# A two-layer network on one core: a first norm shared with VectorE, memsets spread over turns, and a reordered end with spread gathers, earlier additions and a reordered last batch

## The chip, the core and the metric

The kernel runs on one core of a Trainium2 chip. Five engines work side by side, each with its own instruction queue that runs in order: PE (TensorE, matrix products; its weight loads are listed as PEld), DVE (VectorE), ACT (ScalarE), POOL (GpSimd, which also issues the indirect gathers and scatters) and SP (SyncE, which here only issues DMAs). Engines wait for each other through semaphores. The metric is the device time of one execution in microseconds (us); a comparison uses the median of several runs.

## The reference

The input `x` has 16 sequences of 512 tokens with 128 features, all in float32.

```python
xn = layernorm(x)
x = x + memory0(xn) + ffn0(xn)
xn = layernorm(x)
x = x + attention1(xn) + experts1(xn)
```

- `memory0` cuts the sequences into 8 chunks of 64 tokens. Three gate weights give per chunk `alpha`, `theta`, `eta` (a product of each chunk's 64 x 128 values with a 3-column weight). A two-layer memory is trained through the 8 chunks, one after the other, by gradient steps with clipping, and then read by all tokens.
- `ffn0` is a convolution, attention with 16 heads, a norm, 8 experts applied to all tokens and weighted by a softmax, and a norm.
- `attention1` is causal attention with 16 heads, whose output goes through a convolution and becomes the queries of a second causal attention over the same keys and values.
- `experts1` routes each token to 8 of 32 experts; each expert takes the first 128 tokens that chose it, and its weighted outputs are added to those tokens.

## The kernel before

**Turns.** The order of the work is written out by hand. Every stage (the norm, the training scan, one batch's front, one slot's first or second pass over the scores, the experts) is a Python generator, and `Turns.run` advances each live stage by one step per turn, in order of priority (0 first). A stage is listed with the turn in which it begins, and it also waits for marks that others leave (`after`, `mark`), for locks (`acquire`), for free score slots or value tiles (`take`), and for room among three shared PSUM tiles (`room`, `hold`, `drop`). PE's instructions run exactly in that order; on the other engines the framework may reorder what doesn't depend. `fill` adds idle-time products at the end of a thin turn. What matters for the time is thus how many turns there are and how long each takes.

**Attention.** `tops` is the first pass over the scores of one slot (a slot has half the heads of a batch): scores on PE, row maxima on DVE (L387, L395, L396), in the lock `p1`. `back` is the second: scores again with the maxima subtracted, exponential on ACT (L461), in layer 1 the causal mask on POOL (L465), and the product with the values (`pc`), in the lock `p2`. In layer 1 each takes 11 turns per slot, there are four slots a batch (two rounds of two), and a new batch begins every 44 turns (`TBB`). `between(b)` makes the second round's queries from the first round's result. `last(b)` makes the attention's output `xo` and stores it in `ao[b]`.

**The head.** `norm0` normalizes the 16 batches, one begun per turn: `moments` (statistics on DVE, `rsqrt` on POOL, L203 and L204), the scaling in `layernorm` on POOL (L226, four instructions a batch), a transposition into `xnT` on PE, and a store to `xt[0]`. Then the gates: `pg` adds up 64 products, each with 128 columns of `xnT` (every 64th token) as the weights and three columns of `w3` as the moving side. Before all this, three score slots (`qx` zeroed on DVE, L628; `kx` set to one on POOL, L313) and two value tiles (`vp`, L302) are set up. `front0(b)` loads `xt[0, b]` and makes queries, keys and values of layer 0.

**The order after it.** The scan of the memory follows norm0 and must end before layer 1 begins; layer 1 counts its turns from `t0 = max(turns.turn, 480)`. When the routing of the last batch is done, `moe` begins: a placement (four products `pt` over a table of counts, with several DVE instructions each), 32 gathers of a row of counts per expert (L1279) with a count on DVE, and 16 pairs of experts. `fetch` loads a pair's weights on SP and gathers its tokens on POOL (L1314); `pair` runs them through the expert and scatters the result with addition into `acc` in DRAM (L1356), two scatters in one turn. When all pairs are done, `total(b)` loads `acc` and `ao` of each batch (L1381, L1383), adds them on POOL (L1385) and stores the output (L1386), as soon as `ao[b]` is there. The tiles of `total` share a ring of three buffers (tag `hTe`, two tiles a batch); the tiles of `last` share a ring of two (tag `st`) with `front1` and `between`.

Of the kernel before, what the change touches and what calls it, by code (L numbers as in the profile page):

```python
# [82 lines left out]
def network(ctx: ExitStack, tc: tile.TileContext, a, out):  # L83
# [83 lines left out]
    def drop():  # L167

        read[0] += 1
# [49 lines left out]

    def layernorm(dst, src, gain=None, shift=None):  # L220

        got = []
        yield from moments(src, got)
        mv, rs = got[0]
        for t in range(TB):
            nc.gpsimd.tensor_scalar(  # L226
                dst[:, t, :], src[:, t, :], mv[:, t, 0:1], rs[:, t : t + 1], ALU.subtract, ALU.mult
            )
# [71 lines left out]
    def padded_values(pool, i):  # L300
        vp = pool.tile([P, TB, HEADS, 32], F32, bufs=1, name=f"vp{i}")
        nc.gpsimd.memset(vp, 0.0)  # L302
# [4 lines left out]
        return vp  # L307

    def key_rows(pool, i):


        kx = pool.tile([P, NH, S], FR, bufs=1, name=f"kx{i}")
        nc.gpsimd.memset(kx.bitcast(F32), 1.0)  # L313
        return kx

# [308 lines left out]

    def score_slot(pool, i):

        q = pool.tile([P, NH, S], FR, bufs=1, name=f"qx{i}")
        nc.vector.memset(q.bitcast(F32), 0.0)  # L628
        return q, key_rows(pool, i), topd[i]

    free_slots = [score_slot(att, i) for i in range(3)]
    free_values = [padded_values(att, i) for i in range(2)]
    th = const.tile([P, NT, NC], F32, name="th")
# [9 lines left out]
    def norm0(p0):  # L643
# [5 lines left out]
        C0 = Pack(load(p0, "const0", [P, sum(CONST0.values())]), CONST0)  # L649
        xnT = p0.tile([P, N], F32, bufs=1, name="xnT")  # L650

        def one(b):
            xb = p0.tile([P, TB, D], F32, tag="xb", bufs=8, name="xb")
            nc.sync.dma_start(xb, x_b[b])
            yield from layernorm(xb, xb)
            yield from room()
            transpose_tokens(xnT[:, b * S : (b + 1) * S], xb)
            nc.sync.dma_start(xt[0, b], xnT[:, b * S : (b + 1) * S])
            mark("xn", b)
            yield  # L660
# [4 lines left out]
        yield from room()  # L665
        pg = hold("pg")
        for t in range(CHUNK):
            mm(pg[:, 0:3], x_bct[:, :, t], w3[:, t, :], start=(t == 0), stop=(t == CHUNK - 1))
            if t % 8 == 7:
                yield  # L670
        g3 = p0.tile([P, 3], F32, bufs=1, name="g3")
        nc.vector.tensor_copy(g3, pg[:, 0:3])
        drop()
        gr = p0.tile([P, 80], F32, bufs=1, name="gr")
# [340 lines left out]
    def front0(b):  # L1015
        z = live[0, b] = {}
        yield from after(("xn", b))
        xT = fa.tile([P, S], F32, tag="st", bufs=2, name="xT")
        nc.sync.dma_start(xT, xt[0, b])
        yield from idle(2)  # L1020
# [79 lines left out]
    )  # L1100
    with tc.tile_pool(name="p0", bufs=1) as p0:
        stage = norm0(p0)
        turns.stages.append((0, 3, ends(stage, "norm0")))
        turns.run(until=lambda: ("norm0",) in done)
# [9 lines left out]
    row.update(load_rows(l1, "rowsB", ROWSB), caus=C1("caus"), tri=C1("tri"))  # L1114
    free_slots.append(score_slot(l1, 3))
    free_values.append(padded_values(l1, 2))
    pools["pairs"] = False

# [95 lines left out]
    def last(b):  # L1214
# [14 lines left out]
        drop()  # L1229
        nc.sync.dma_start(ao[b], xo)  # L1230
        mark("ao", b)
        yield

    istar = mw.tile([P, EXP1], F32, name="istar")
    base = mw.tile([P, EXP1], F32, name="base")
# [3 lines left out]
    def moe(mo):  # L1239
# [10 lines left out]
        per = 512 // NTILE  # L1250
        for u in range(EXP1 // per):
            es = slice(u * per, (u + 1) * per)
            bd = ff.tile([EXP1, per, NTILE], F32, tag="ew1", bufs=2, name="bd")
            nc.vector.tensor_tensor(bd, bc(cur, 1, per), bc(memE[:, es], 2, NTILE), ALU.mult)
            yield from room()
            pt = work("pt")
            mm(pt, ones[0:EXP1, :], bd.rearrange("k e i -> k (e i)"))
            ptv = pt.rearrange("p (e i) -> p e i", i=NTILE)
            le = ff.tile([P, per, NTILE], F32, tag="ew2", bufs=2, name="le")
            nc.vector.tensor_scalar(le, ptv, col("iota"), None, ALU.is_le)  # L1260
            nc.vector.tensor_reduce(istar[:, es], le, AX.X, ALU.add)
            nc.vector.tensor_tensor(le, le, ptv, ALU.mult)
            nc.vector.tensor_reduce(base[:, es], le, AX.X, ALU.max)
            yield
        nc.vector.tensor_scalar(base, base, -1.0, col("iota"), ALU.mult, ALU.add)
# [11 lines left out]
        for e in range(EXP1):  # L1277
# [7 lines left out]
            if e >= 8:  # L1285
                count(e - 8)
            if e % 2 == 1:
                yield
        for e in range(EXP1 - 8, EXP1):
            count(e)  # L1290
        yield
        nc.vector.scalar_tensor_tensor(tok, istar, float(P), tok, ALU.mult, ALU.add)
# [12 lines left out]
        def fetch(e2):  # L1305
# [4 lines left out]
            nc.sync.dma_start(dn, a["dn"][:, es, :])  # L1310
            xg = mo.tile([P, 2, XW], F32, tag="xg", bufs=3, name="xg")
            for i in range(2):
                e = 2 * e2 + i
# [4 lines left out]
                )  # L1318
            return gu, dn, xg

        def pair(e2, gu, dn, xg):
# [19 lines left out]
            nc.vector.tensor_tensor(he, he, pgs[:, 1], ALU.mult)  # L1341
            yield
            yield from room()
            peo = toks(hold("peo")[:, 0 : 2 * D])
# [9 lines left out]
            for i in range(2):  # L1354
                e = 2 * e2 + i
                nc.gpsimd.indirect_dma_start(  # L1356
                    out=acc, out_offset=bass.IndirectOffsetOnAxis(ap=sidx[:, e : e + 1], axis=0),
                    in_=eo[:, i, :], in_offset=None,
                    bounds_check=N + P - 1, oob_is_err=True, compute_op=ALU.add,
                )  # L1360
            yield

        ahead = [fetch(0), fetch(1)]
        yield from idle(2)
        going = []
        for e2 in range(EXP1 // 2):
            going.append(pair(e2, *ahead.pop(0)))
            if e2 + 2 < EXP1 // 2:
                ahead.append(fetch(e2 + 2))
            for _ in range(3):  # L1370
                going = [g for g in going if next(g, StopIteration) is not StopIteration]
                yield
        while going:
            going = [g for g in going if next(g, StopIteration) is not StopIteration]
            yield
        mark("moe")

    def total(b):
        yield from after(("moe",), ("ao", b))
        x1 = ff.tile([P, TB, D], F32, tag="hTe", bufs=3, name="fin")  # L1380
        nc.sync.dma_start(x1, acc_b[b])  # L1381
# [133 lines left out]
```

## Time and profile before

| | |
|---|---|
| median of 3 runs | 4081.94 us |
| lowest, highest | 4064.09, 4087.86 us |
| the profiled execution | 4071.58 us |
| its span | 4069.8 us |
| mean granted PE clock | 0.952 |
| busy: PE | 3646.2 us (90%) |
| DVE | 2368.5 us (58%) |
| ACT | 2201.1 us (54%) |
| POOL | 1681.3 us (41%) |
| DMA traffic | 374.22 MB |

The span is what the profiler saw from the first to the last instruction; the execution's own time is 1.8 us more. A busy share is a mean over stages with different limits, so the stretches at the start and at the end are read by themselves: busy time per window, the timeline (each row: start, length, engine, line, operation, what is written and read, and in brackets how long the engine was idle before it and what ended that), and the chain of waits, which follows the last instruction back to what released it. The clock column is the share of full clock that PE was granted.

### The profile page before, as it was taken

The numbers are of one execution on the slowest core, as the hardware profiler recorded it, in microseconds if no ns is written. First come the engines' busy times: TensorE is split into PE (matmuls) and PEld (weight loads), VectorE is DVE, ScalarE is ACT, GpSimd is POOL, SyncE is SP. The second block draws the span as 40 slices with busy tenths as digits, with TensorE's granted clock in tenths as the row PEclk, the third lists the DMA queues.
The fourth block names the chain that finished last, engine by engine and source line by source line (L and its number), as shares of the span: only waits on it lengthen the run. The fifth ranks groups of instructions, "written<-read, shape, count | busy, mean of one in ns | idle before, by whom it ended". The sixth has DMA issues, their size and how long they took to land.

```text
span 4069.8 us, 62831 instructions
## 1 busy us (share of the span) xinstructions
PE 3646.2 (90%) x22668; PEld 1974.2 (49%) x22668; DVE 2368.5 (58%) x5165; ACT 2201.1 (54%) x3686; POOL 1681.3 (41%) x2598
## 2 busy tenths in 40 slices
PE   5998899888999998999999999999999999987877
PEld 2544454444544444455555555555555555543443
DVE  3575656665565555564566655666656666676651
ACT  1355655566557775555555555555555555542332
POOL 7334534455333544134333442333334423434563
PEclk6799999999999999999999999999999999997888
DMA  4222222122223333333333333333333343323334
GB/s 155 62 62 62 70 57 77 57 68 64 75 75 93 108 96 108 101 105 110 90 111 103 114 81 111 108 100 95 111 101 107 87 117 106 94 69 98 70 69 131
DMA packets 271222, 374.22 MB, mean 92 GB/s; under 512 B 42392, under 2 KB 116800, under 8 KB 270144
## 3 DMA queue, kind: packets, MB, share of 16 engines
q1 hardware_dynamic: 263744, 363.38, 30.7%
q0 software_dynamic: 7168, 6.82, 1.0%
q8 instruction: 180, 2.95, 0.3%
q14 instruction: 130, 1.06, 0.1%
HBM read 236.85 MB, written 133.25 MB: 91 GB/s over the span
## 4 chain that ended last, share of the span: by engine, by line
PE 62%; DVE 15%; POOL 7%; ACT 6%; DMA 5%; issue 5%; SPq 0%; POOLq 0%; ACTq 0%; DVEq 0%
PE s L190 16%; PE pye L573 10%; PE phe L190 9%; PE pc L190 9%; DVE nm L396 7%; DVE s L395 3%; ACT e L461 2%; PE pgr L190 2%; POOL e L465 1%; PE tp L241 1%; DVE s L387 1%; PE fill L197 1%; PE po L190 1%; PE pj L190 1%; DMA fin<-ao 1%
## 5 line engine op out<-in xcount | busy, mean ns | idle before, releaser
L461 ACT ACTIVATE e<-s 128x1024 f32<-128x1024 f32 (+1 forms) x1216 | 1190.6, 979 | 836.5 <-PE s L190 796.0
L396 DVE TENSOR_REDUCE nm<-s 128x2 f32<-128x1024 f32 (+1 forms) x704 | 861.9, 1224 | 664.6 <-PE s L190 657.5
L387 DVE CUSTOM_DVE_ANT_0 s<-s,sb_const 128x512 f32<-128x512 f32 (+1 forms) x1024 | 647.6, 632 | 663.9 <-PE s L190 646.4
L465 POOL TENSOR_SCALAR_AFFINE_SELECT e<-e 128x128 f32<-128x128 f32 (+2 forms) x1408 | 464.4, 363 | 1140.9 <-ACT e L461 1133.0
L190 PE MATMUL s<-kx,qx 64*128 64x512 f32 (+3 forms) x3072 | 627.6, 435 | 180.9 <-DVE nm L396 99.4
L190 PE MATMUL pc<-e,vp 128*32 128x512 f32 (+3 forms) x6144 | 712.4, 511 | 52.4 <-POOL e L465 51.3
L190 PEld LDWEIGHTS s<-kx,qx 64*128 64x128 f32 x3072 | 278.7, 189 | 754.0 <-issue 288.9
L573 PEld LDWEIGHTS pye<-ew,hTe 128*128 128x128 f32 x4096 | 517.2, 193 | 212.1 <-issue 195.6
L573 PE MATMUL pye<-ew,hTe 128*128 128x128 f32 x4096 | 572.7, 283 | 0.5 <-DVE cn L486 0.5
L190 PE MATMUL phe<-x1T,ew 128*128 128x512 f32 x1024 | 553.5, 624 | 6.9 <-DVE vp L345 1.9
L190 PE MATMUL s<-qx,kx 64*128 64x512 f32 (+3 forms) x3072 | 536.1, 373 | 21.1 <-ACT e L461 15.3
L565 ACT ACTIVATE hTe<-phe,sb_cols 128x512 f32<-128x512 f32 x512 | 353.1, 690 | 272.5 <-PE phe L190 272.1
L190 PEld LDWEIGHTS s<-qx,kx 64*128 64x128 f32 x3072 | 290.7, 190 | 124.2 <-issue 64.6
L581 POOL TENSOR_TENSOR ac<-ac,y 128x512 f32<-128x512 f32 x128 | 165.4, 1292 | 387.0 <-ACT y L580 386.8
L395 DVE TENSOR_TENSOR s<-s,sb_const 128x256 f32<-128x256 f32 (+1 forms) x384 | 199.4, 519 | 178.8 <-PE s L190 166.5
L190 PEld LDWEIGHTS pc<-e,vp 128*32 128x32 f32 x6144 | 137.6, 109 | 264.7 <-issue 152.2
L190 PEld LDWEIGHTS phe<-x1T,ew 128*128 128x128 f32 x1024 | 158.2, 193 | 113.3 <-issue 84.6
L580 ACT ACTIVATE y<-pye,pr 128x128 f32<-128x128 f32 x512 | 146.8, 368 | 51.0 <-PE pye L573 50.0
L387 DVE DVE_READ_ACCUMULATOR2_ANT nm<- 128x1 f32 x1024 | 145.0, 142 | 0.0
L197 PE MATMUL fill<-sb_pb,sb_const 128*128 128x512 f32 (+3 forms) x256 | 135.9, 621 | 8.8 <-DMA sb_pb<-in_pb 7.8
L437 ACT COPY cs<-pc 128x512 f32<-128x512 f32 x96 | 56.2, 585 | 61.1 <-PE pc L190 59.4
L410 ACT CAST m<-tpm 16x512 fp32r<-16x512 f32 x96 | 54.6, 569 | 59.4 <-PE tpm L408 59.4
(285 smaller groups left out, 4049.0 us busy)
## 6 DMA issues: line engine op xcount, KB each, us to landing
ew<-in_ew SPq DMA_DIRECT2D x256, 256.0 KB
kx<-rk SPq DMA_DIRECT2D x192, 256.0 KB
qx<-rq SPq DMA_DIRECT2D x128, 256.0 KB
rq<-hi SPq DMA_DIRECT2D x64, 256.0 KB
rq<-lo SPq DMA_DIRECT2D x64, 256.0 KB
rk<-hi SPq DMA_DIRECT2D x64, 256.0 KB
rk<-lo SPq DMA_DIRECT2D x64, 256.0 KB
qx<-r SPq DMA_DIRECT2D x64, 256.0 KB
```

The lines of the kernel that those rows point to most:

```text
L190: nc.tensor.matmul(o, lhsT=lhsT, rhs=rhs, start=start, stop=stop)
L197: nc.tensor.matmul(o[:, 0:n], lhsT=ident, rhs=cell[0][:, 0:n], start=True, stop=True)
L387: newest[0] = nc.vector.tensor_tensor_reduce(out=sv[:, r, 0, :], in0=sv[:, r, 0, :], in1=row["caus"][:, S - n :], scale=1.0, scalar=-BIG, ...
L395: nc.vector.tensor_tensor(dg, dg, bc(row["caus"][:, S - P :], 1, per), ALU.add)
L396: newest[0] = nc.vector.tensor_reduce(nm[:, qt, :, t : t + per], sv, AX.X, ALU.max)
L437: nc.scalar.copy(cs, got[0])
L461: nc.scalar.activation(e[:, :, 0 : per * n], s[:, :, 0 : per * n], AF.Exp, scale=SCALE)
L465: cleared[0] = nc.gpsimd.affine_select(out=ev[:, r, :, 0:P], in_=ev[:, r, :, 0:P], pattern=[[0, per], [1, P]], compare_op=ALU.is_ge, fill= ...
L565: nc.scalar.activation(hs[i], ph, AF.Relu, bias=col("fb", i))
L573: nc.tensor.matmul(pye[0][:, t, :], lhsT=h[:, t * P : (t + 1) * P], rhs=w2[e][:, f, :], start=(f == 0 and t == 0), stop=(f == 3), skip_gro ...
L580: nc.scalar.mul(y[:, t, :], pye[0][:, t, :], pr[:, t, e : e + 1])
L581: nc.gpsimd.tensor_tensor(ac, ac, y, ALU.add)
```

## The change

**Head.** The x loads of the first four batches are given priority over other loads. The scaling of the first norm runs on DVE for batches 0 to 3, and alternates between DVE and POOL for the others. The three slots and two value tiles are set up by stages that begin in turns 0, 8, 22 (slots 0, 1, 2: POOL, DVE, POOL) and 2, 24 (values), not before turn 0. `front0(0)` reads `xnT` in place. The gate product swaps its sides: `w3`'s three columns are the weights, and the 128 columns of `xnT` move; the result is copied, transposed back and copied. Slot 3, set up before layer 1, is set on POOL alone.

```diff
-    def layernorm(dst, src, gain=None, shift=None):
+    def layernorm(dst, src, gain=None, shift=None, on=None):
...
-            nc.gpsimd.tensor_scalar(
+            (on or (nc.gpsimd,))[t % len(on or (0,))].tensor_scalar(
...
+    def ready_slot(slot, on):
+        for t, value in zip(slot, (0.0, 1.0)):
+            on.memset(t.bitcast(F32), value)
+            yield
+        free_slots.append(slot)
+
+    fresh = [score_slot(att, i, (nc.gpsimd, nc.vector, nc.gpsimd)[i]) for i in range(3)]
+    fresh += [padded_values(att, i) for i in range(2)]
...
-            nc.sync.dma_start(xb, x_b[b])
-            yield from layernorm(xb, xb)
+            with ExitStack() as first:
+                if b < 4:
+                    first.enter_context(tc.high_priority())
+                nc.sync.dma_start(xb, x_b[b])
+            yield from layernorm(xb, xb, on=(nc.vector,) if b < 4 else (nc.vector, nc.gpsimd))
...
-        pg = hold("pg")
+        pg = hold("pg")[0:3, 0:P]
         for t in range(CHUNK):
-            mm(pg[:, 0:3], x_bct[:, :, t], w3[:, t, :], start=(t == 0), stop=(t == CHUNK - 1))
+            mm(pg, w3[:, t, :], x_bct[:, :, t], start=(t == 0), stop=(t == CHUNK - 1))
...
+        gT = p0.tile([3, P], F32, bufs=1, name="gT")
+        nc.scalar.copy(gT, pg)
+        drop()
+        yield
+        yield from room()
+        pgt = work("pg3")[:, 0:3]
+        nc.tensor.transpose(pgt, gT, ident[0:3, 0:3])
         g3 = p0.tile([P, 3], F32, bufs=1, name="g3")
-        nc.vector.tensor_copy(g3, pg[:, 0:3])
-        drop()
+        nc.vector.tensor_copy(g3, pgt)
...
+        turns.stages += [(t, 2, stage) for t, stage in zip((0, 8, 22, 2, 24), fresh)]
```

**Experts.** Each of the four placements becomes a stage of four steps, and the four start one turn apart. The gathers of counts come three in two turns where they came two in one, and the last eight counts in two turns. The gathers and the scatters of a pair come one a turn, and a pair has one more idle turn before its second product.

```diff
-        for u in range(EXP1 // per):
+        def places(u):
...
             nc.vector.tensor_tensor(bd, bc(cur, 1, per), bc(memE[:, es], 2, NTILE), ALU.mult)
+            yield
             yield from room()
-            pt = work("pt")
+            pt = hold("pt")
...
+            yield
             nc.vector.tensor_scalar(le, ptv, col("iota"), None, ALU.is_le)
             nc.vector.tensor_reduce(istar[:, es], le, AX.X, ALU.add)
+            yield
             nc.vector.tensor_tensor(le, le, ptv, ALU.mult)
+            drop()
             nc.vector.tensor_reduce(base[:, es], le, AX.X, ALU.max)
-            yield
+        yield from side(*[places(u) for u in range(EXP1 // per)])
...
-            if e % 2 == 1:
+            if e % 3 != 0:
                 yield
         for e in range(EXP1 - 8, EXP1):
             count(e)
-        yield
+            if e % 4 == 3:
+                yield
+        mark("counted")
...
             for i in range(2):
                 e = 2 * e2 + i
+                if i == 1:
+                    yield
                 nc.gpsimd.indirect_dma_start(
                     out=acc, out_offset=bass.IndirectOffsetOnAxis(ap=sidx[:, e : e + 1], axis=0),
```

**Additions.** A batch whose attention output is ready before `counted` is added to `acc` at once, and `total` then copies it from `acc` to the output, DRAM to DRAM.

```diff
-        nc.sync.dma_start(ao[b], xo)
+        if ("counted",) in done:
+            nc.sync.dma_start(ao[b], xo)
+        else:
+            x2 = l1.tile([P, TB, D], F32, tag="st", bufs=2, name="xs")
+            nc.sync.dma_start(x2, acc_b[b])
+            yield from idle(2)
+            nc.gpsimd.tensor_tensor(x2, x2, xo, ALU.add)
+            nc.sync.dma_start(acc_b[b], x2)
+            whole.add(b)
...
         yield from after(("moe",), ("ao", b))
+        if b in whole:
+            nc.sync.dma_start(out_b[b], acc_b[b])
+            return
```

**The last batch.** Its stages begin 12 to 24 turns earlier than its place in the row of batches, and so come into the list of stages before some of batches 13 and 14.

```diff
+    def begun(b, i, c):
+        early = 0 if b < B - 1 else 12 if i else 16 + 8 * c
+        return t0 + b * TBB + 20 + 66 * i + 11 * c - early
...
-        + [(t0 + b * TBB + 20 + 66 * i + 11 * c, 0, tops(1, b, i, c)) for b in range(B) for i in range(2) for c in range(2)]
-        + [(t0 + b * TBB + 40 + 66 * i + 11 * c, 1, back(1, b, i, c)) for b in range(B) for i in range(2) for c in range(2)]
-        + [(t0 + b * TBB + 60, 4, between(b)) for b in range(B)]
+        + [(begun(b, i, c), 0, tops(1, b, i, c)) for b in range(B) for i in range(2) for c in range(2)]
+        + [(begun(b, i, c) + 20, 1, back(1, b, i, c)) for b in range(B) for i in range(2) for c in range(2)]
+        + [(begun(b, 0, 0) + 40, 4, between(b)) for b in range(B)]
```

More of the change, by code (lines that the diff above doesn't have):

```diff
@@ L301, in padded_values, with ready_values @@
         vp = pool.tile([P, TB, HEADS, 32], F32, bufs=1, name=f"vp{i}")
+        return ready_values(vp)
+    def ready_values(vp):
         nc.gpsimd.memset(vp, 0.0)
@@ L306, in padded_values @@
             )
[L307 to L314, printed above, removed]
+        free_values.append(vp)
+        yield
     def split_rows(p, bias, order, dst):
@@ L623, in network, with score_slot @@
     row.update(load_rows(fa, "rows0", ROWS0))
-    def score_slot(pool, i):
+    free_slots, free_values = [], []
+    def score_slot(pool, i, on):
         q = pool.tile([P, NH, S], FR, bufs=1, name=f"qx{i}")
[L628 to L632, printed above, removed]
+        k = pool.tile([P, NH, S], FR, bufs=1, name=f"kx{i}")
+        return ready_slot((q, k, topd[i]), on)
+    def ready_slot(slot, on):
[5 more added lines that the diff above has]
+    fresh += [padded_values(att, i) for i in range(2)]
     th = const.tile([P, NT, NC], F32, name="th")
@@ L650, in norm0 @@
         xnT = p0.tile([P, N], F32, bufs=1, name="xnT")
+        live["xnT"] = xnT
         def one(b):
             xb = p0.tile([P, TB, D], F32, tag="xb", bufs=8, name="xb")
-            nc.sync.dma_start(xb, x_b[b])
-            yield from layernorm(xb, xb)
+            with ExitStack() as first:
[3 more added lines that the diff above has]
+            yield from layernorm(xb, xb, on=(nc.vector,) if b < 4 else (nc.vector, nc.gpsimd))
             yield from room()
@@ L1017, in front0 @@
         yield from after(("xn", b))
-        xT = fa.tile([P, S], F32, tag="st", bufs=2, name="xT")
-        nc.sync.dma_start(xT, xt[0, b])
-        yield from idle(2)
+        if b == 0:
+            xT = live["xnT"][:, 0:S]
+        else:
+            xT = fa.tile([P, S], F32, tag="st", bufs=2, name="xT")
+            nc.sync.dma_start(xT, xt[0, b])
+            yield from idle(2)
         yield from room()
@@ L1114, in network @@
     row.update(load_rows(l1, "rowsB", ROWSB), caus=C1("caus"), tri=C1("tri"))
-    free_slots.append(score_slot(l1, 3))
-    free_values.append(padded_values(l1, 2))
+    for _ in score_slot(l1, 3, nc.gpsimd):
+        pass
+    for _ in padded_values(l1, 2):
+        pass
     pools["pairs"] = False
@@ L1229, in last @@
         drop()
-        nc.sync.dma_start(ao[b], xo)
+        if ("counted",) in done:
+            nc.sync.dma_start(ao[b], xo)
+        else:
+            x2 = l1.tile([P, TB, D], F32, tag="st", bufs=2, name="xs")
+            nc.sync.dma_start(x2, acc_b[b])
+            yield from idle(2)
+            nc.gpsimd.tensor_tensor(x2, x2, xo, ALU.add)
+            nc.sync.dma_start(acc_b[b], x2)
+            whole.add(b)
         mark("ao", b)
         yield
+    whole = set()
     istar = mw.tile([P, EXP1], F32, name="istar")
@@ L1311, in fetch @@
             xg = mo.tile([P, 2, XW], F32, tag="xg", bufs=3, name="xg")
+            ahead.append((gu, dn, xg))
             for i in range(2):
@@ L1318, in fetch @@
                 )
-            return gu, dn, xg
+                yield
         def pair(e2, gu, dn, xg):
@@ L1342, in pair @@
             yield
+            yield
             yield from room()
@@ L1355, in pair @@
                 e = 2 * e2 + i
+                if i == 1:
+                    yield
                 nc.gpsimd.indirect_dma_start(
@@ L1361, in pair @@
             yield
-        ahead = [fetch(0), fetch(1)]
+        ahead, going = [], [side(fetch(0), fetch(1))]
         yield from idle(2)
[L1365 to L1373, printed above, removed]
+        at = e2 = 0
+        while going or e2 < EXP1 // 2:
+            if at % 3 == 2 and e2 < EXP1 // 2:
+                going.append(pair(e2, *ahead.pop(0)))
+                if e2 + 2 < EXP1 // 2:
+                    going.append(fetch(e2 + 2))
+                e2 += 1
             going = [g for g in going if next(g, StopIteration) is not StopIteration]
+            at += 1
             yield
```

## The prediction

> **What bounds it now.** The page first: one core, span 4069.8 us, execution 4071.58 us, against a median of 4081.94 us of three runs (4064.09 to 4087.86), so the sums below start 10 us under the median.
>
> ```profile
> PE   5998899888999998999999999999999999987877
> POOL 7334534455333544134333442333334423434563
> PEclk6799999999999999999999999999999999997888
> PE 62%; DVE 15%; POOL 7%; ACT 6%; DMA 5%; issue 5%; SPq 0%; POOLq 0%; ACTq 0%; DVEq 0%
> ```
>
> In the middle PE is busy nine tenths at nearly full clock; the change adds no PE work there. The first slice and a half and the last four have idle PE, low clock and busy POOL, and all edits but small ones lie there. The order of the code is in turns, and L461 issues one exponential per turn while a second pass runs: matching those rows with the walk of the stages dates every turn. Norm0 ends in turn 31 (132 us), the scan in 481, `xw` of batch 15 in 1167 (3680 us), `moe` in 1243 (3967 us), the last second pass in 1275.
>
> **The head.** Busy time by stretch (length, then busy us and count of PE, PEld, DVE, ACT, POOL; clock, DMA share, GB/s), then POOL's timeline:
>
> ```profile
> 16.00:88.00 72.00, 37.04 (x91) 16.99 (x91) 21.02 (x100) 10.57 (x18) 67.24 (x92) 0.55 0.44 143
> 92.00:131.00 39.00, 39.00 (x156) 32.92 (x156) 12.94 (x15) 0.30 (x2) 0.19 (x1) 0.50 0.15 46
> 84.15 0.19 POOL L203 TENSOR_SCALAR rs_t<-ln_mv 128x4 f32<-128x4 f32 x1
> 84.42 1.02 POOL L204 TENSOR_TENSOR ln_rs<-rs_t,nhalf 128x4 f32<-128x4 f32 x1
> 85.55 3.12 POOL L226 TENSOR_SCALAR xb<-xb,ln_mv,ln_rs 128x128 f32<-128x128 f32 x4
> ```
>
> Until 88.7 us POOL sets the pace: 4.6 us a batch. Then until 131 us PE does, in the gate product `pg`: eight turns of 16 passes, 3.56 us each lot in the chain, at half clock though it is busy all the time.
>
> **The tail.** The same columns, five stages:
>
> ```profile
> 3590.00:3680.00 90.00, 78.33 (x528) 36.47 (x528) 65.47 (x177) 41.16 (x50) 34.33 (x84) 1.00 0.29 83
> 3682.00:3713.00 31.00, 17.18 (x51) 5.52 (x51) 20.77 (x48) 3.37 (x5) 2.17 (x8) 0.56 0.21 55
> 3713.00:3781.00 68.00, 53.99 (x295) 23.14 (x296) 45.40 (x160) 22.23 (x26) 49.18 (x74) 0.87 0.33 83
> 3781.00:3965.00 184.00, 148.34 (x888) 79.04 (x886) 98.30 (x260) 71.67 (x109) 113.99 (x162) 0.82 0.34 72
> 3965.00:4070.00 105.00, 76.06 (x332) 31.77 (x332) 22.70 (x54) 24.81 (x29) 35.10 (x61) 0.80 0.43 128
> ```
>
> Before `moe` a turn takes 2.6 us; in the placement (3682 to 3713) 6.5 to 11, in the gathers 3.4, in the expert pairs 3.67 (50 turns, 3781.2 to 3964.7), and after it 2.6 under the chain of final additions. Why a pair turn is long, in the timeline of one bad turn:
>
> ```profile
> 3796.47 1.63 POOL L1356 DMA_INDIRECT acc<-eo,sidx  x1 [0.31 <-issue]
> 3800.01 1.56 POOL L1356 DMA_INDIRECT acc<-eo,sidx  x1 [1.26 <-DMA acc<-eo,sidx]
> 3802.28 0.65 PE L190 MATMUL pc<-e,vp 128*32 128x128 f32 x6 [2.84 <-POOL e L465]
> 3803.80 1.02 ACT L461 ACTIVATE e<-s 128x1024 f32<-128x1024 f32 x1 [8.57 <-PE s L190]
> ```
>
> The second scatter of a pair waits on POOL for the first one's landing (3.3 us); the masks L465 of the second pass stand behind it, PE behind them, and ACT idles 8.57 us. The end, from the chain of waits:
>
> ```profile
> 3974.93 2.89 DMA fin<-ao
> 3977.95 1.27 POOL fin L1385
> ...
> 4057.75 0.70 DVE xo L1228
> 4058.47 2.01 DMA ao<-xo
> 4060.54 2.54 DMA fin<-ao
> 4063.21 1.29 POOLq L1511
> ```
>
> Sixteen times a load and an addition, two loads ahead at most, with the masks of the last batch in the same POOL queue.
>
> **Head edits, summed.** Four x loads go ahead of seven constant loads on SP: issued at 0.8 us instead of 4.4, landed by about 5 (`pb`, issued 3.0, was used at 7.8), where the first statistics ran at 10.75. The constants move back 1.7 us on SP, under the first norm. The memsets of slots 1, 2 and `vp1` (1.8 us a piece) leave the front: slot 1 goes to DVE in turn 8, the rest to POOL in turns 22 and 24, where POOL is busy 0.19 of 39 us; they are needed from turn 20 and 32 on. Slot 3's q memset goes from DVE to POOL, 1.8 us near 1576 us, not on the path. First norm: four batches leave POOL only L203 and L204 with gaps, 1.3 us; twelve leave 1.3 + 2 x 0.79 + 0.1 = 3.0. POOL then ends at 6 + 4 x 1.3 + 12 x 3.0 = 47 us; DVE's 40 new scalings are not in the trace in this shape; the nearest, `he` L1339 at 96x256, takes 0.28, so about 0.2 each, and DVE was busy 21 of 72 us. **A rule against this edit**: the Trainium skill, SBUF — State Buffer, Who interferes with whom, says that a DVE tensor_scalar in a two-port mode and a GpSimd instruction exclude each other on a shared port pair. L1339 ranges from 0.23 to 0.75 us, which could be that; L226 has no such spread (0.78 to 0.80), but met no DVE scaling. By the row nothing is added; by the rule, as an estimate, each of 24 scalings costs POOL 0.2, 5 us. I take 3, and 2 more for DVE queued behind L396, which in before waited 10.8 us for the first scores: last norm at 52 us, against 88.7: **-36**.
>
> Gate product: the three gate columns become the weights and 128 tokens the moving side; as many passes (128). Nearest row: `pgu` (96 columns, 128 moving), 8 passes in 1.04 us at full clock, 1.95 at half: 0.13 or 0.24 a pass, against 0.22 now. **Rule two**: TensorE: Matmul & The Clock Gate, Part 1, has the clock open after about 3.4 us of busy PE. The row above denies it for this product (39 of 39 us busy, 0.50), so three moving columns do not count as work; whether 128 do over three weight columns no row shows. `pc` with 32 weight columns runs at full clock. By the rule a turn is 16 x 0.13 + 0.4 for scores = 2.5 us and eight, with a cold start, 24 us against 34: -10; by the half-clock row 37: +3. I take -10, as the wide moving side resembles `pc`. The turned product adds a copy, a transpose, and **one turn** (about 2 us here). Batch 0's front no longer waits for its `xt` load (4.9 us on PE) and comes two turns earlier, under POOL. Head: -36 - 10 + 2 = **-44**, ends +3 on the clock, +5 on the port: -44 to -26. Since later turns hold the same work, this carries to the end. The later norm makes the scan end in 482, and as layer 1 starts at the larger of that and 480, everything there is a turn late: +2.6.
>
> **Tail edits, by turns.** Placement: four products, each stepped over four turns and staggered, are eight turns (1168 to 1176), not four; `pt` no longer waits on PE in the turn that makes `bd` (7.7 us in the first). DVE adds 4 x (0.68 + 1.44 + 1.37) = 14 us to 8 x 2.1, the wait for the pool's change stays: 36 us. The pool slots `pt` now holds are at most two at a turn's start, so the maxima still find room. Gathers: 1.5 a turn at 1.3 us with gap, plus 0.75 of masks, is 2.75 of POOL, under PE's 2.6 to 3: 28 turns to the first pair, at 3.0: 84. Pairs: scatters one a turn; start to start 3.5 to 4.0 us when they wait, so turns near 3 leave a wait under 1 us. POOL needs 2 x 1.35 + 2 x 1.6 + 3 x 0.75 = 8.2 us in three turns. At 3.2: 46 turns, 147. Moe then ends near 1257. The last batch's begin turns come before batch 13's second round: its rows are ready in 1167, it waits for score lock ahead of that round, so the four passes of round one end 11 turns earlier, its second round begins at once after batch 14's, and the gap of 18 turns at the last slot becomes 11: last second pass at 1269. From 1250, 7 turns with pairs (2.4) and 12 with second passes alone (2.1): 42. The end from there stays: 16.4 (transposes, `xo`, `ao` out, in, addition, store).
>
> Final additions: batches 0 to 12 have `ao` before `counted` (batch 12 at 1162, counted at 1199), so add during layer 1: a load, a POOL addition of 1.27 and a store each, every 44 turns, where POOL was busy 34 of 90 us; at the end 13 copies of 256 KB. At the tail's rate (128 GB/s at a share of 0.43, so 298) that is 11 us, under 40 us of second passes. Cover gone, they'd cost those 11.
> Sum from 3682: 36 + 84 + 147 + 42 + 16 + 3 for the turn = 328, end at 4010: **-60**.
>
> **Forecast.** 4071.6 - 44 - 60 = 3968; on the median's footing up to 3978. I say **3970**, own range 3945 to 3995: chance 0.52.
>
> **Rivals.** (a) The scatter chain, not its bunching, sets the pairs: every scatter still waits for the landing of the last, turns stay 3.67 and gathers 3.4. Against: L1356 waited for a landing only 12.0 us in all; for: PE waited 31.5 us on masks. +22 +11: **4003**, chance 0.18. (b) Clock stays half and the port locks: +13 +5: **3990**, 0.14. (c) Masks undelayed and clock full let pair turns fall to the 2.6 of before `moe`: -28: **3942**, 0.10. (d) Slower: `xs` takes a third place in the `st` ring of two buffers, just where the next batch's `xT` sits until its value product, 13 us later (3408 to 3421 for batch 10); its load would stand on SP ahead of the row stores and weight loads. From 130 us gain and margin over 13 batches it decides at 10 us a batch; all 13 us lost gives **4140**. Against: no maxima load fell due in that stretch, and the rows have turns to spare. 0.04. That the edits don't take effect: 0.02, 4075.
>
> A difference under 0.5% (20 us) can't be told from none. Faster 0.93, same 0.03, slower 0.04; range 3928 to 4022, which takes in (a), (b), (c).
>
> **What would show it.** L226 on DVE and POOL, last before 55 us; `pg` passes near 0.13 and clock 1.0 there; norm0 near 88 us. In the tail pair turns near 3.2, no ACT idle of 8 us, the fin chain three long, and the last `xo` some 100 us earlier. Wrong if SP waits at the `xs` load, or head gains vanish by 300 us.

## The result, and the profile after

The changed kernel took 4028.53 us (median of 4 runs, 4017.65 to 4029.9), the kernel before 4079.29 us beside it. The ratio is 0.9866 [0.9845, 0.9888]: faster by 1.3%, some 51 us, where 3970 us (109 us less than 4079) had been forecast, and 6.5 us above the top of the wider range (3928 to 4022). The profiled execution took 4017.65 us (its span 4015.9 us), so it stands 54 us under that of before and 50 us over the sum of 3968 made for the same footing.

First the page of the changed kernel: the 40 slices and the chain by engine.

```profile
PE   5889989898999889999999999999999999998886
POOL 5433553354334454134333433443333344333664
PEclk7999999999999999999999999999999999998898
PE 64%; DVE 14%; POOL 7%; ACT 5%; issue 5%; DMA 4%; SPq 1%; POOLq 0%; ACTq 0%; DVEq 0%
```

POOL's first digits fall from 7, 3, 3 to 5, 4, 3, the clock of the second slice goes from 7 to 9, and PE's last six slices read 998886 where they read 987877. SP's queue, 0% of the chain before, now has 1%. The same view by stretch (columns as in the prediction: busy us and count of PE, PEld, DVE, ACT, POOL; clock, DMA share, GB/s):

```profile
80.00:90.00 10.00, 10.00 (x47) 4.19 (x46) 2.45 (x2) 0.00 (x0) 0.00 (x0) 1.00 0.30 103
3782.00:3953.00 171.00, 136.95 (x844) 72.59 (x846) 97.33 (x260) 67.05 (x105) 105.13 (x150) 0.90 0.33 71
3953.00:3977.00 24.00, 18.39 (x121) 9.06 (x114) 3.83 (x10) 9.49 (x14) 12.97 (x20) 0.93 0.21 29
3977.00:4016.00 39.00, 22.53 (x124) 9.59 (x122) 1.48 (x3) 8.37 (x10) 11.09 (x22) 0.84 0.56 157
```

In the first row the gate product runs at full clock (1.00 against 0.50), but the 47 products in these 10 us are 41 of its 128 passes and six score products. The second row is the pairs with 46 turns: 171 us, with PE still idle for 34 of them. The third row is the last eight turns with pairs, and the fourth what follows `moe`: 39 us, where before the row of 105 us stood. Dates of turns, from the exponentials, with the working turn by turn (the rows go by turn number; in after the last batch's `xw` is made in turn 1169, in before in 1167, so that at its store after leads by only 4.2 us, 3678.0 against 3682.2):

| stage (turns of after) | forecast | measured in after | before |
|---|---|---|---|
| last scaling of the first norm ends | 52 us | 72.6 us | 88.7 us |
| gate product (20 to 28) | 24 us | 30.6 us | 32.7 us |
| date of turn 32 | about 92 us | 115.9 us | 135.9 us |
| date of turn 1168 | 44 us earlier | 12.9 us earlier (3668.7) | 3681.6 us |
| placement (1168 to 1176) | 36 us | 35.3 us | |
| gathers (1176 to 1204) | 84 us | 78.6 us | |
| pairs (1204 to 1250) | 147 us, 3.2 a turn | 170.7 us, 3.71 a turn | 3.67 a turn, 50 turns |
| turn 1250 to the end of the span | 58.4 us | 62.6 us | |

The missing 50 us are thus 31 up to turn 1168 (20.6 in the norm, 6.6 in the gate product, some 4 between it and the tail) and 19 in the tail (pairs +23.7, end +4.2, placement and gathers -6.1, less 2.6 that were booked for an extra turn).

**The norm.** Four queues of after around 40 us, from its timeline (start, length, engine, line, operation, in brackets the idle time before and what ended it): POOL, DVE, PE, and SP's DMA issues.

```profile
35.92 0.79 POOL L227 TENSOR_SCALAR xb<-xb,ln_mv,ln_rs 128x128 f32<-128x128 f32 x1
46.82 0.19 POOL L203 TENSOR_SCALAR rs_t<-ln_mv 128x4 f32<-128x4 f32 x1 [10.11 <-DVE ln_mv L213]
...
45.51 0.49 DVE L212 BATCH_NORM_STATS2 ln_st<-xb 128x6 f32<-128x128 f32 x2 [5.62 <-DMA xb<-in_x]
...
51.01 1.23 DVE L394 TENSOR_REDUCE nm<-s 128x2 f32<-128x1024 f32 x1 [2.19 <-PE s L190]
...
48.02 0.76 PE L190 MATMUL s<-kx,qx 64*128 64x512 f32 x1 [8.61 <-DMA kx<-rk]
...
40.02 0.90 SPq L328 DMA_DIRECT2D rk<-lo  x2
40.97 0.55 SPq L669 DMA_DIRECT2D xt<-xnT  x1
41.61 0.60 SPq L665 DMA_DIRECT2D xb<-in_x  x1
```

POOL, which was to be the pace, stands idle for 10.1 us. DVE has no statistics for it, since the next batch's `x` was issued on SP only at 41.6 us, behind batch 0's row stores; and right behind that, PE's first score product waits 8.6 us for the key rows, which go out to DRAM and back, with DVE's first maxima behind it. The kernel before had that same wait, in DVE's timeline:

```profile
67.88 1.23 DVE L396 TENSOR_REDUCE nm<-s 128x2 f32<-128x1024 f32 x1 [10.76 <-PE s L190]
```

Two things thus hold up the statistics in after: the late `x`, which the forecast does not have, and the first scores, which it puts at 2 us.

**The pairs.** One turn of after's pairs in the timeline (POOL, PE and DVE):

```profile
3841.71 1.09 POOL L1358 DMA_INDIRECT xg<-xw,gidx  x1 [0.30 <-DVE nm L385]
3843.10 1.05 POOL L1358 DMA_INDIRECT xg<-xw,gidx  x1 [0.31 <-issue]
3844.17 0.77 POOL L463 TENSOR_SCALAR_AFFINE_SELECT e<-e 128x256 f32<-128x256 f32 x2
3844.63 1.43 PE L190 MATMUL pc<-e,vp 128*32 128x256 f32 x8 [4.13 <-POOL e L463]
...
3849.58 0.57 DVE L385 CUSTOM_DVE_ANT_0 s<-s,sb_const 128x384 f32<-128x384 f32 x1 [8.15 <-PE s L190]
```

The code now issues one gather a turn, yet POOL runs both back to back ahead of the mask, as it does for all 13 pairs that are gathered while others run: they write the same buffer of a ring of three (tag `xg`), and both are released together, when the pair that held it has made its last reading (L1397); experiment 9 tests this. The mask stands behind them, PE 4.13 us behind the mask, and DVE 8.15 us behind PE, which does the pair's own products in between.

### The profile page after: what moved, and what is told of

Same layout as the page of the kernel before. It is cut to its first block, busy times and chain, and to the rows that moved or that the text cites. A ratio compares the mean times of both kernels' runs of the same rounds, so it can differ in the third digit from the quotient of the medians.

```text
span 4015.9 us, 62757 instructions
## 1 busy us (share of the span) xinstructions
PE 3599.7 (90%) x22665; PEld 1942.9 (48%) x22665; DVE 2379.9 (59%) x5203; ACT 2200.3 (55%) x3687; POOL 1655.0 (41%) x2560
## 3 DMA queue, kind: packets, MB, share of 16 engines
q1 hardware_dynamic: 266720, 359.71, 31.1%
## 4 chain that ended last, share of the span: by engine, by line
PE 64%; DVE 14%; POOL 7%; ACT 5%; issue 5%; DMA 4%; SPq 1%; POOLq 0%; ACTq 0%; DVEq 0%
PE s L190 16%; PE phe L190 10%; PE pye L571 10%; PE pc L190 9%; DVE nm L394 7%; DVE s L393 2%; ACT e L459 2%; PE pgr L190 2%; PE tp L242 1%; DVE s L385 1%; POOL e L463 1%; PE fill L197 1%; PE po L190 1%; PE pq L190 1%; DMA xT<-xt 1%
## 5 line engine op out<-in xcount | busy, mean ns | idle before, releaser
L190 PE MATMUL pc<-e,vp 128*32 128x512 f32 (+3 forms) x6144 | 702.4, 508 | 40.7 <-POOL e L463 39.5
L197 PE MATMUL fill<-sb_pb,sb_const 128*128 128x512 f32 (+3 forms) x252 | 124.8, 583 | 10.5 <-DMA zrow<-zero 10.0
L435 ACT COPY cs<-pc 128x512 f32<-128x512 f32 x96 | 56.3, 586 | 58.4 <-PE pc L190 55.7
L203 POOL TENSOR_SCALAR rs_t<-ss 128x4 f32<-128x4 f32 (+1 forms) x56 | 11.0, 197 | 165.8 <-ACT sq L256 164.0
```

The costliest lines, as they stand in the source:

```text
L190: nc.tensor.matmul(o, lhsT=lhsT, rhs=rhs, start=start, stop=stop)
L197: nc.tensor.matmul(o[:, 0:n], lhsT=ident, rhs=cell[0][:, 0:n], start=True, stop=True)
L435: nc.scalar.copy(cs, got[0])
```

## The experiments

Each ratio is to runs of the kernel before on the same chip; differences of a few us between medians are at the edge of what can be told (the intervals are 7 to 28 us wide).

**1 and 2. Each half alone.** `head_only` keeps the first norm, the fills and the gate product of the change and takes the functions of the tail from before; `tail_only` the reverse.

> The head of the change alone, the end as before. Theory A (the head gave less than forecast: norm0 ends some 16 us earlier and two turns more, about 2.6 us each, take a third of it back): 8 to 14 us faster than before, near 4067 us. Theory B (the whole 20 us that turn 32 shows carry to the end): 20 us faster, near 4059. The prediction's own sum: 41 us faster, near 4038.

> The end of the change alone, the head as before. Theory A: 40 to 46 us faster than before, near 4036 us. Theory B: 30 to 34 us faster, near 4047. The prediction's own sum: 60 us faster, near 4019. If head and end act on different turns, the two gains add up to the gain of the change (51 us by the medians).

Measured: `head_only` 4065.62 us, ratio 0.9978 [0.9967, 0.9988]: 9 us by the ratio, 11 by the medians. `tail_only` 4039.8 us, 0.9915 [0.9899, 0.9932]: 35 and 37 us, between its two theories. So the head is worth about 10 and not 44; the tail gives most of the gain, though not the 60 of the forecast. By the medians the halves add up to 48 of the 51 us, the same within the noise. In the traces, from the last store of `xw` to the end, the tail gains somewhat more: 342.8 us in `tail_only` and 337.9 in after, against 387.6 before.

**3 and 4. Two parts of the tail taken out.**

```diff
-        early = 0 if b < B - 1 else 12 if i else 16 + 8 * c
+        early = 0
```

> The changed kernel with the last batch in its place in the row. By the turns the last second pass then ends 6 turns later. Theory A (after the pairs the second passes set the end, 1.7 us a turn): 10 to 12 us slower than the changed kernel. Rival (the pairs of experts and the copies set the end): no difference, below 3 us.

```diff
-        if ("counted",) in done:
+        if True:
             nc.sync.dma_start(ao[b], xo)
```

> The changed kernel with all 16 additions left to the end. Theory A (the chain of load and addition, 4 to 5.5 us a batch, begins when the pairs end at 3977 us and is the last thing): 16 batches need 70 to 88 us from there, end near 4055, 35 to 48 us slower than the changed kernel. Rival (the last batch's second passes, which still need 39 us from there, cover most of it and the early additions cost as much in layer 1): under 20 us slower.

Measured: `no_overtake` 4030.4 us, 0.9892 [0.9874, 0.991]; by the median 2 us more than after, by the trace 6.5 us more from the last `xw` (turn 1169) to the end (349.5 against 343.0). The overtaking is worth 2 to 7 us, less than the 10 to 12 of Theory A; more can't be told. `no_early_add` 4069.04 us, 0.9978 [0.9968, 0.9988]: 40 us more than after. Of the tail's gain nearly all hangs on the additions made ahead: without them the chain of final additions, one every 5 us, sets the end again and hides whatever the placement, the gathers and the pairs save. Two links of it, from the chain of waits of `no_early_add`:

```profile
4022.90 1.27 POOL fin L1435
4024.60 2.96 DMA fin<-ao
4027.72 1.27 POOL fin L1435
```

**5 to 8. One suspected cost each.** Sixteen places for `xb` in place of eight, so that no x load waits for a place and is issued behind the row stores:

> The changed kernel with 16 x buffers for 8, so that no x load waits for a buffer and then stands on SP behind the row stores of batch 0. Theory A (the loads of batches 9 to 15 set the norm's end): the last L227 of the first norm ends 10 to 15 us before the 72.6 us of the changed kernel and DVE no longer waits 5.6 us for an x tile; the time falls by as much, 0.3%. Rival (the row stores and loads fill the DMA engines between 40 and 50 us in any case): the last L227 moves by less than 4 us.

The gate product over 128 neighbouring columns of `xnT` in place of every 64th, which adds up other tokens (so the gates of the memory are other numbers) in as many passes:

```diff
-            mm(pg, w3[:, t, :], x_bct[:, :, t], start=(t == 0), stop=(t == CHUNK - 1))
+            mm(pg, w3[:, t, :], xnT[:, t * P : (t + 1) * P], start=(t == 0), stop=(t == CHUNK - 1))
```

> The changed kernel with the gate product's moving side read from 128 neighbouring columns and not from every 64th (so the gates are other numbers, and all that depends on them). Theory A (the stride of 256 bytes is what a pass of 0.21 us pays at full clock): a pass falls to 0.11 to 0.13 us, the eight turns from 31 to 17 to 20 us. Rival (a pass with three weight columns has this price whatever the stride): still 0.2 us a pass.

The gathers and scatters of a pair two a turn, as before, with the rest of the change:

> The changed kernel with both gathers and both scatters of a pair in one turn again, and without the idle turn before the second product. Theory A (spreading them gave nothing, since POOL's order still puts them together: 3.71 us a turn in the pairs against 3.67 before): within 5 us of the changed kernel, pair turns 3.5 to 3.9. The prediction's step: pair turns rise by 0.5 us, some 20 us slower.

And the tokens fetched by SP from fixed rows, in place of POOL's indirect gather (so the experts get other tokens):

```diff
-                nc.gpsimd.indirect_dma_start(
-                    out=xg[:, i, :], out_offset=None, in_=xw,
...
-                yield
+                nc.sync.dma_start(xg[:, i, :], xw[e * P : (e + 1) * P, :])
+                yield
```

> The changed kernel with the tokens of each pair loaded by SP from fixed rows instead of gathered on POOL (so the experts get other tokens). Theory A (the gathers ahead of the masks in POOL's queue hold up the second passes): pair turns fall from 3.71 to 3.0 to 3.2, some 25 us faster. Rival (the scatters' landings, or PE at half clock, set the pair turn): pair turns above 3.5, under 8 us faster.

Measured:

| run | us | ratio to before | what its trace shows |
|---|---|---|---|
| `xb16` | 4018.49 | 0.9848 [0.9814, 0.9882] | norm ends at 69 us; turn 32 at 111.8 (after: 115.9) |
| `pg_contig` | 4010.37 | 0.9825 [0.9797, 0.9852] | gate turns 2.52 us (3.83); turn 32 at 103.5 |
| `pairs_bunched` | 4019.06 | 0.9852 [0.9825, 0.9879] | pair turns 3.73 us (3.71) |
| `plain_gather` | 3998.86 | 0.9798 [0.9772, 0.9825] | pair turns 3.04 us |

`xb16` removes the wait for `x`, and the wait behind it comes forward: DVE then idles 10 us for the first scores, and the norm gains 4 us, not 10. From the waits of `xb16` up to 80 us (us in total, times, longest):

```profile
DVE nm L394 <- PE s L190: 15.5, 5, 9.7
```

`pg_contig` shows where the gate product's gain stayed. The rows of its passes in after and in `pg_contig` (duration in ns least/median/most, then first and last start in us; overlapping passes, so the pace is the distance of the starts):

```profile
L190 PE MATMUL pg<-xnT,sb_const x128: 374/393/397, 78.0 to 109.1; 128*3 128x128 f32 x128
```

```profile
L190 PE MATMUL pg<-xnT,sb_const x128: 272/273/418, 77.8 to 96.9; 128*3 128x128 f32 x128
```

Same count, same shape: 31.1 us from first to last start over columns 256 bytes apart, at a granted clock of 1.00, and 19.1 us over neighbours, at 0.92, so the clock is not the cause. A pass, score products included, takes 0.24 and 0.15 us; the expectation had 0.11 to 0.13 for the second. (The 12 us by turn 32 are shown; that the median is 18 us lower than after's is within its interval of 22.) `pairs_bunched` says that spreading the instructions over turns, the edit itself, brought nothing to the pairs (from the last store of `xw` to the end this run takes 332.8 us, after 337.9), and `plain_gather` that POOL's gathers are what makes them long.

**9. A fourth place in the ring of gathered tokens** (the memory comes from one of the 12 places for the gathered counts):

```diff
-            xg = mo.tile([P, 2, XW], F32, tag="xg", bufs=3, name="xg")
+            xg = mo.tile([P, 2, XW], F32, tag="xg", bufs=4, name="xg")
```

> The changed kernel with four buffers for the gathered tokens where there were three (and 11 for the counts where there were 12, to make room). With three, both gathers of a pair wait for the same buffer, which the pair before the last gives up only when its outputs are scaled, so POOL takes them back to back ahead of the masks, though the code gives each a turn. Theory A (this bunching makes the pair turn 3.7 us): pair turns fall to 3.1 to 3.3, 18 to 26 us faster than the changed kernel. Rival (POOL's time in the gathers counts, wherever they stand): pair turns stay above 3.5, below 8 us.

Measured: 4003.54 us, 0.982 [0.9803, 0.9838]; pair turns 3.17 us. The pairs of `xg4` in POOL's timeline and, below, as a stretch:

```profile
3839.56 1.06 POOL L1358 DMA_INDIRECT xg<-xw,gidx  x1 [0.17 <-issue]
3842.06 0.54 POOL L463 TENSOR_SCALAR_AFFINE_SELECT e<-e 128x128 f32<-128x128 f32 x2 [1.44 <-ACT e L459]
3842.87 1.59 POOL L1403 DMA_INDIRECT acc<-eo,sidx  x1 [0.27 <-issue]
3845.55 0.53 POOL L463 TENSOR_SCALAR_AFFINE_SELECT e<-e 128x128 f32<-128x128 f32 x2 [1.09 <-ACT e L459]
3846.31 1.05 POOL L1358 DMA_INDIRECT xg<-xw,gidx  x1 [0.23 <-issue]
```

```profile
3782.00:3929.00 147.00, 126.56 (x853) 69.28 (x856) 100.24 (x263) 67.02 (x105) 106.27 (x150) 0.93 0.38 82
```

Now gather, mask, scatter, mask, gather alternate, as the code has them (of those 13 pairs none has its two gathers back to back, in after all have), and 46 turns take 146 us. The waits of the stretch, first after, then `xg4`:

```profile
PE pc L190 <- POOL e L463: 23.4, 13, 4.1
POOL acc L1403 <- DMA acc<-eo,sidx: 5.2, 5, 1.5
```

```profile
PE pc L190 <- POOL e L463: 8.1, 11, 2.5
POOL acc L1403 <- DMA acc<-eo,sidx: 4.2, 5, 1.4
```

PE's wait for masks falls from 23.4 to 8.1 us while POOL does the same work (105 and 106 us). The scatters' wait for a landing, rival (a) of the prediction, is 5.2 and 4.2 us: it had stopped mattering in after already.

**10 to 12. The norm freed of the first scores.** `tops_late` is `xb16` with the first score pass of batch 0 begun in turn 20; `head_all` also ties the three fills left on POOL behind the last scaling; `best` adds the fourth place of `xg`. The output of these three differs from that of after for a reason that was not found; they serve to read the norm and the turns, and are no versions to use.

```diff
-        + [(b * TA + 4 + 16 * c, 0, tops(0, b, 0, c)) for b in range(B) for c in range(2)]
+        + [(b * TA + (4 if b else 20) + 16 * c, 0, tops(0, b, 0, c)) for b in range(B) for c in range(2)]
```

> The 16 x buffers, and the first score pass of batch 0 begun in turn 20 instead of 4, after the first norm. Theory A (DVE holds the later batches' statistics behind the first maxima, which wait some 9 us for the key rows; with that gone POOL sets the pace): last L227 of the first norm near 56 to 60 us against 72.6 in the changed kernel and 68.5 with 16 buffers alone, no wait of POOL over 3 us; about 12 us off at turn 20. Rival (the DMA engines are full then in any case): last L227 above 65 us.

> As the run before, and the memsets of slot 2 and of the second value tile held behind the last scaling of the first norm on POOL, where their turns 22 and 24 mean them (the order of turns binds PE alone, and POOL took them between 6 and 17 us). Theory A: POOL reaches the scaling of batch 4 some 5 us sooner (22.3 us in the changed kernel), and the last L227 falls by as much again, to 51 to 55 us. Rival (x loads and statistics are not there sooner): less than 2 us.

> All of these together: four token buffers, 16 x buffers, the first score pass begun after the norm, late memsets. Theory A: the gains add, 35 to 45 us faster than the changed kernel, near 3988 us. Rival (the head's gain goes again in the layers, as 9 of 16 us did with the head alone): 20 to 28 us, near 4004.

Measured: 4070.79, 4068.73 and 4053.52 us (0.9984 [0.9975, 0.9993], 0.9976 [0.9966, 0.9986], 0.9929 [0.9903, 0.9954]). `tops_late` has the norm done at 58.9 us (`xb16`: 68.6), within its Theory A, and the scaling rows of `head_all` show it done at 55.1 us, close to the 52 of the forecast:

```profile
L229 POOL TENSOR_SCALAR xb<-xb,ln_mv,ln_rs x24: 784/832/870, 18.8 to 54.3; 128x128 f32<-128x128 f32 x24
```

Turn 32 comes at 94.8 us, 41 us before the kernel before. And yet the end is 40 us later than after's: the scan ends in turn 488 in place of 483, layer 1 takes 3.14 us a turn in place of 3.08 (turns 483 to 1000), the last batch no longer overtakes, and the last second pass is in turn 1281 in place of 1270. The five turns by which layer 1 begins later are some 16 us, less than the 21 gained at turn 32; the longer turns cost the rest (from the start of layer 1 to the last `xw` 686 turns take 2149 us, in after 2101). So the place of the maxima is the cause of the norm's stall, but moving them is no remedy; why the turns are longer stays open.

**13 and 14. The fills alone, and with the fourth place.** `xb16` with only the fills tied behind the last scaling; then with `xg` of four.

> After with 16 places for the x tiles and with the three fills of the change that POOL still does in the head (key rows, query rows, values; 1.8 us each) tied behind the last scaling in its issue order; batch 0's first score pass stays where it is. Theory A (the scheduler puts the fills on POOL ahead of the norm's scalings although their turns are 22 and 24, so the norm ends later by what they hold up): the last scaling ends about 3 us before that of the run with 16 places alone (68.5 us there, so 65 to 66), turn 32 is earlier by 2 to 4 us, and the median is 4014 to 4019, about 3 us under the 4018.5 of that run. Rival B (the first scalings wait for batch statistics, and the 9 to 10 us in which DVE stands behind the first maxima set the end of the norm whatever POOL has done): the last scaling stays at 68 to 69 us and the median within 4016 to 4022; the fills only move behind the norm and may then hold the first score passes of batch 1, which would show as a later turn 32.

> The same kernel with the fourth place for the gathered tokens. Theory A: the head's gain and the tail's do not touch each other, so the time is that of the fourth place alone, 4003.5, less what the head saves against after (10 us for the 16 places by the medians, 4 by the date of the last scaling, and 0 to 3 for the fills): 3990 to 3999, with pair turns of 3.1 to 3.2 us. Rival B: a head that is earlier is lost again before the tail, as in the two runs whose first score pass was moved, and the time stays at 4002 to 4006.

Measured: `memsets_late` 4025.03 us, 0.988 [0.9859, 0.99], `xg4_memsets_late` 3998.29 us, 0.981 [0.9791, 0.9829]. Rival B in the first: POOL begins the shared batches 3 us earlier and then waits 13.1 us in place of 9.4; the last scaling starts at 68.4 us (68.2 in `xb16`), and turn 32 falls back to 116.0. So the fills, which the framework pulls ahead of the norm although their turns are 22 and 24, were not what held the norm. Why turn 32 is later is in the timeline of `memsets_late`, DVE and POOL:

```profile
68.36 5.62 DVE L229 TENSOR_SCALAR xb<-xb,ln_mv,ln_rs 128x128 f32<-128x128 f32 x1
...
68.62 1.80 POOL L642 MEMSET qx<- 128x2048 f32 x1
70.37 1.80 POOL L642 MEMSET kx<- 128x2048 f32 x1
72.11 1.80 POOL L311 MEMSET vp<- 128x2048 f32 x1
```

A DVE scaling of 0.34 us (the median of its row) lasts 5.62 us and ends when the third fill does, so that the norm ends at 74.0 us (68.6 in `xb16`).

**15 and 16. The 13 copies at the end.** In after SP issues them in one piece, before the loads for the last three additions; the timeline of after, SP and DVE:

```profile
3980.19 9.64 SPq L1428 DMA_DIRECT2D out<-acc  x13
3989.87 0.77 SPq L1431 DMA_DIRECT2D fin<-acc  x1
...
4003.34 0.49 SPq L1256 DMA_DIRECT2D ao<-xo  x1
...
3998.72 0.69 DVE L1252 TENSOR_TENSOR xo<-po,sb_rowsB 128x512 f32<-128x512 f32 x1 [2.64 <-PE po L190]
```

The last `xo` is made at 3999.4 us, but its store waits on SP until 4003.3, behind the stores and loads of the additions that the copies held up.

```diff
         if b in whole:
+            yield from idle(2 + b // 2)
             nc.sync.dma_start(out_b[b], acc_b[b])
```

> After, with the 13 copies of finished batches put two a turn from the third turn behind moe on, in place of all in one turn. Theory A (the copies are not hidden, as the prediction had it: in after their issues hold SP for 9.6 us ahead of the loads for batch 13's addition, that addition comes 9 us late, and the store of batch 15's attention output stands on SP 4 us behind batch 13's and 14's stores and loads): batch 13's addition no longer waits for the copies, the store of batch 15's output follows its making at 0.5 us or less in place of 3.9, and the time from the last xo to the end falls from 16.5 to 12 to 13.5 us; the median is 3 to 6 us under after's 4028.5, too little for a verdict by the median alone, so the trace decides. Rival B (the chain before is set by the last second passes, and the 4 us are only shifted): xo to end stays at 16 to 17 us, median 4024 to 4033.

> The fourth place for the gathered tokens and the spread copies. Theory A: from the last xo (3974.8 us in the run with the fourth place alone) to the end 16.7 us become 12 to 13.5, the median 3997 to 4001. Rival B: end unchanged, median 4000 to 4006.

Measured: 4024.98 us (0.9873 [0.9855, 0.9891]) and 4001.99 us (0.982 [0.9801, 0.984]). From the start of the last `xo` to the end of the span it is now 12.4 us (4002.65 to 4015.0) and 12.1, in place of 17.2 and 16.7: Theory A. The same queues in `copies_spread`:

```profile
3991.88 6.92 SPq L1429 DMA_DIRECT2D out<-acc  x9
4003.37 0.34 SPq L1256 DMA_DIRECT2D ao<-xo  x1
...
4002.65 0.69 DVE L1252 TENSOR_TENSOR xo<-po,sb_rowsB 128x512 f32<-128x512 f32 x1 [2.65 <-PE po L190]
```

The code has two copies a turn; SP issues two, two and then nine in one piece, but the nine are through at 3998.8 us, before the last `xo` is made, and its store follows at once. The last `xo` itself came 3 to 4 us later in both profiled executions, which were 2.5 to 2.8 us late already at the last store of `xw`, ahead of anything that this edit touches; counted from there the end comes 3.4 and 4.2 us sooner (334.5 against 337.9, 307.2 against 311.4). The medians moved by 3.5 and 1.5 us, too little to tell from none.

The versions with the fourth place (4003.5, 3998.3, 4002.0 us) beat both kernels, by about 2% the one before, and can't be told from one another.

## Why the prediction was wrong, by its own steps

**Direction: right.** Faster by more than 0.5%, with .93 on it, and through the parts named. **Size: half**, for four terms of the sum.

- **"2 more for DVE queued behind L396"** is the term that failed most: what it stands for was 14 us (POOL's idle time among the shared batches, 10.1 us at one place alone). Taken apart, the last scaling at 72.6 is 20.8 us until the shared batches begin, 12 batches and 14 us of gaps. A batch took 3.15 us against a forecast of 3.0, so that term was right. The 10.1 us were the late `x`, a wait that the sum leaves out; with `x` on time (`xb16`) the first scores hold DVE 9.7 us in the same place. The view for that wait was there: the stall of before was 10.8 us, named in the prediction and priced at 2. A faster norm did not shorten it: the first scores wait for batch 0's rows to go out to DRAM and come back.
- **"Memsets leave the front"** was wrong as a fact (a begin turn orders PE, and the other engines take what is ready), and the shared batches began at 20.8 us against 11.2. The fills are only 3 of these 9.6 us (17.6 in `memsets_late`); in after DVE's statistics of batch 4 also waited for `x` until 13.1 us. Ahead of the stall the 3 us cost nothing in the end, as `memsets_late` shows; with the stall gone, moving the fills was worth 4 us at the norm's end (58.9 in `tops_late`, 55.1 in `head_all`).
- **"As many passes ... 0.13 a pass"** took the pace of `pgu`, whose moving side is contiguous. The question that was weighed, whether the clock opens, was answered as forecast (1.00); the one that wasn't asked, how the 128 columns lie, cost 0.24 us a pass with the score products in between, against 0.15. The Trainium skill, SBUF — State Buffer, in Door 1: The DMA port swizzle, has 16-byte lines and a penalty for each access to a new one; at 256 bytes every column is one. That rule spoke against this pace and was not used. What the stride costs here is 12 us, by `pg_contig`; that the lines are the reason was not shown, since no other stride was run.
- **"Pairs at 3.2"**: 3.71. The sum of POOL's work, 8.2 us in three turns, was not too low (105 us busy in 46 turns are 6.9), and 3.2 is what `xg4` reached. What failed is "scatters one a turn" as the cure: the bunch that mattered in after was the two gathers, released together by the ring. Rival (a) had the time of the pairs (3.67) with the wrong mechanism.
- **"Cover gone, they'd cost those 11"** looked at the copies' transfer, which was covered. Their issue on SP was not: 9.6 us, of which 4 to 5 came out at the end.
- **Right**: the additions ahead (40 us by `no_early_add`), placement (36 against 35.3), gathers (84 against 78.6), the number of turns within one or two, and rival (d): turns 484 to 1000 take 3.08 us each in after, before 3.09, so the `xs` loads hold up nothing that counts.
- **Open**: between turns 32 and 1168 after lost 7 us of its lead, and as its `xw` is made two turns later, not one, 3 us more count against it than were booked. It is lost in layer 0: from turn 37 to the first turn of layer 1 after takes 447 turns and 1447 us, before 445 and 1432. Executions of programs that are the same up to turn 1145 (`no_overtake`, after) differ by 19 us at turn 1166, so the rest is not attributed.

## What to carry to other kernels

Spreading instructions over a hand-written order did nothing here, where a ring of buffers released them together: look at what each waits for before counting what each costs, and try one more buffer first. When an engine is relieved, price the next queue by the whole wait that stands in it today, not by a remainder; and count the issues of DMAs, not only their bytes, on the queue that the last store has to pass. When the pace of a product is taken from another row, compare the access pattern too, not only the shape.

## What the runs showed of the hardware that was not expected

- Three weight columns with 128 moving columns ran at full clock (1.00 over 80 to 90 us), which the forecast had left open, where 128 weight columns with three moving ones stayed at 0.50 though PE was busy 39 of 39 us.
- 128 float32 moving columns 256 bytes apart against neighbours: 31.1 us (clock 1.00) against 19.1 (0.92) from the first to the last of 128 passes, score products included.
- In three places a DVE scaling lasted until POOL's fills ended: 5.62 us in `memsets_late` (three fills one after the other, so it was not let in between two), 1.47 in `xb16` and 0.98 in after, both ending at 17.3 us with a fill that ran from 15.42 to 17.22, against a median of 0.33. The Trainium skill, SBUF — State Buffer, Who interferes with whom, has the exclusive lock; the prediction had asked what POOL would lose to DVE, and the larger loss was DVE's; that the lock is the reason is argued from these three, not tested. POOL's scalings beside DVE's rose only from 0.79 to 0.86 us, where the estimate had 0.2 each.
